# Output projection of a grouped attention as seven block products, with its weights and partial sums restaged

## The chip, the core and the metric

The kernel runs on one core of one Trainium2 chip. The metric is the device time of one execution in microseconds. A core has the engines TensorE (PE in the profile, its weight loads PEld), VectorE (DVE), ScalarE (ACT), GpSimd (POOL) and SyncE (SP, which here only issues DMAs).

## The reference

One block works on x of 1024 tokens by 512 channels, all float32: x plus attention A (32 heads of 16), plus a feed-forward with routed low-rank experts, plus attention B, plus the same feed-forward again. The change lies in attention B, which has 32 query heads and 8 key/value heads of 128 channels:

```python
q = (x @ Wq.T).reshape(b, s, H, HD).transpose(0, 2, 1, 3)
k = (x @ Wk.T).reshape(b, s, HKV, HD).transpose(0, 2, 1, 3)
v = (x @ Wv.T).reshape(b, s, HKV, HD).transpose(0, 2, 1, 3)
q = _rmsnorm(q, q_norm_w)
k = _rmsnorm(k, k_norm_w)
...
attn = jax.nn.softmax(scores + bias[None], axis=-1)
out = jnp.einsum('bkgqs,bksd->bkgqd', attn, v)
out = out.reshape(b, H, s, HD).transpose(0, 2, 1, 3).reshape(b, s, H * HD)
return out @ Wo.T
```

The mask is causal, with a slope per head. The last line, `out @ Wo.T`, is the output projection: 1024 x 4096 times 4096 x 512.

## The kernel before, in words

Attention B (`attention_b`, from L743) walks over 8 groups g, one per key/value head, with four query heads hh each. For one head, `softmax` (L1070) makes eight row tiles of 128 queries, i from 7 down to 0. A tile's scores go by PE into the two score banks (`s`, L1079, up to 1024 columns in pieces of 512), DVE adds scale and bias (L1081) and takes the maximum (L1085), ACT makes the exponentials (L1088), DVE the reciprocal of the sum (L1090), POOL the division (L1091). Two tiles later (`LAG = 2`) `columns` has DVE transpose the tile in 32x32 blocks (L1106, L1112). After a head's last tile, `product` (L1154) has PE multiply by v into the four banks `o` in strips of 32 partitions (L1140); the part of keys 512 to 1023 of all four heads is done once per group in `product_rest` (`or`), at the third tile of the next group. ACT copies the result to `oT` (L1173), 128 channels by 1024 tokens for each head, in five buffers.

All other PE work of attention B is cut into units and mixed between the tiles. The main loop (L1266 on) lets a tile's PE work be followed by as many units as `due` says, from the table `SHARE`. n counts the 32 tiles of a group. A unit is always worth one 128x512 product, which is two PE instructions in float32. In group g these run, in this order (`parts`):
- `project_kv(g + 1)`, 14 units: k and v of the next group, 128-column products (L920). With x and the weights cut into 2 x 2 blocks, `seven` (L868) makes four block products out of seven; ACT copies two of the seven out of PSUM (L880, L883), DVE adds the other five (L888), and POOL makes the sums of weight blocks that serve as weights (L862, L865, L881, L884). The next product into a bank has to wait until the previous one was read out, and the order `STEADY` leaves another product between the two.
- `project_o(g - 1)`, 32 units (L760): for each of eight token tiles four 128x512 products, summed in one bank over the four heads (L765). ACT copies each sum to one of two slots (`stage`, L772), and POOL issues a DMA that adds it to the running sum xd in HBM (L773). For the last group there is no xd; its two halves are added to x directly (L779, L781).
- `project_q(g + 1, r)`, 14 units for each pair r of heads: 512-column products (L993), `seven` as above.

The two banks `m` (`ps_m`) serve all units, the transposes of k and the sums of squares. `sum_ready` and `square` form the scale of each query head: ACT squares (L1035), PE sums (L1057), DVE transposes (L1063) and scales (L1067), POOL takes the power (L121). They run after `project_kv` and at the ends of heads.

Weights have a buffer each: `wkv` (512 KB, L797), `wq` (1 MB, L807) and `wo` (1 MB, L814), loaded on SP's queue a group ahead. SP also makes the 32 copies of v per group (L909). The units of a group end with the group (`for _ in fill` at L1326); group 0 has 42, the others 74.

Of the kernel before, what the change touches and what calls it, by code (L numbers as in the profile page):

```python
# [64 lines left out]
class Block:  # L65
# [527 lines left out]
    def load_ffn(self, pools, queue, tags, w_baseT, w_rhT, lora_B, b_base):  # L593
        w = {}
        small = pools[0].tile([P, self.FFN_SMALL], F32, tag=tags[0], name="w_small")
# [4 lines left out]
        w["base"] = pools[1].tile([P, KC, C], F32, tag=tags[1], name="w_base")  # L600
# [142 lines left out]
    def attention_b(self, ctx, wo_pool, WqT, WkT, WvT, WoT, qw, kw, xnT, xd, missing, ffn_weights):  # L743
# [12 lines left out]
        stage = beside[:, 3]  # L756
        wp = ctx.enter_context(tc.tile_pool(name="b_w", bufs=1))
        oTs = {}

        def project_o(g, wo, heads, ps_m, tag, spare=None):  # L760

            for t in range(NT):
# [7 lines left out]
                if g < HKV - 1:  # L770
                    to, rows = stage[:, t % 2], xd[t * P : (t + 1) * P, :]
                    nc.scalar.copy(to, ps)  # L772
                    nc.gpsimd.dma_start(rows, to, accum_op=ALU.add)  # L773
                    if g == HKV - 2:
                        if t == 0:
                            self.hold(self.xp, "o")
                        nc.sync.dma_start(self.x[t], rows)
                elif spare is None:
                    nc.vector.tensor_add(self.x[t], self.x[t], ps)  # L779
                else:  # L780
                    nc.scalar.copy(spare[:, t % 2], ps)  # L781
                    add = nc.gpsimd.tensor_tensor(self.x[t], self.x[t], spare[:, t % 2], ALU.add)
                    if t >= NT - 2:

                        tc.keep_in_program_order(add)
                yield

        with ExitStack() as ctx:
# [7 lines left out]
            def load_kv(g, pinned=False):  # L796
                wkv = wp.tile([P, KC, 2, DB], F32, tag="wkv", name=f"wkv{g}")  # L797
# [8 lines left out]
            def load_q(g, pinned=False):  # L806
                wq = wp.tile([P, KC, GRP * DB], F32, tag="wq", name=f"wq{g}")  # L807
                dma = nc.sync.dma_start(wq, WqT[:, g * GRP * DB : (g + 1) * GRP * DB].rearrange("(k p) n -> p k n", p=P))
# [10 lines left out]
            wkv, wq = load_kv(0, pinned=True), load_q(0, pinned=True)  # L819
# [37 lines left out]
            def weight_forms(w, name, pinned=True):  # L857
# [3 lines left out]
                s2 = work.tile([P, H, DB], F32, tag="s2", name=f"s2_{name}", bufs=3)  # L861
# [6 lines left out]
            def seven(new, multiply, left, c11, c12, c21, c22, order, done, aside=None):  # L868
# [3 lines left out]
                for m in order:  # L872
# [16 lines left out]
                    if m == 7 and aside:  # L889
                        aside()  # L890
# [20 lines left out]
            def project_kv(g, forms, aside=None):  # L911
# [21 lines left out]
                def done():  # L933
                    if not g:
                        loaded.append(load_kv(1))
# [5 lines left out]
                    for half, k_sb in enumerate(halves):  # L941
                        ssq = sm.tile([P, 4], F32, tag="ssq", name=f"ssq{g}_{half}")
                        for a in range(4):
                            sq = work.tile([P, DB], F32, tag="ksq", name=f"ksq{g}_{half}_{a}")
# [11 lines left out]
                    forms,  # L956
# [4 lines left out]
                    aside=aside,  # L961
# [15 lines left out]
            def q_forms(g, wq, r):  # L977
                return weight_forms(wq.rearrange("p k (n d) -> p k n d", d=DB)[:, :, 2 * r : 2 * r + 2], f"q{g}_{r}", g > 0)

            ahead = {}  # L980

            def project_q(g, wq, r, new=None):
# [33 lines left out]
                if g:  # L1016
                    if not r:
                        ahead[g, 1] = q_forms(g, wq, 1)
                    if later:
                        k_columns(*later.pop(0))  # L1020
# [3 lines left out]
                    ahead.pop((g, r)),  # L1024
# [19 lines left out]
            loaded = []  # L1044

            def sum_squares(g, hh, sq_T, behind):
# [15 lines left out]
                by_token = work.tile([P, NT, B], F32, tag="st", name=f"by{g}_{hh}", bufs=1)  # L1062
# [131 lines left out]

            def boundary():
# [5 lines left out]
            wo = load_o(0)  # L1201
            with tc.high_priority(offset=400):
                kv_forms = weight_forms(wkv, "kv0", False)
                for r in range(2):
                    ahead[0, r] = q_forms(0, wq, r)
            front = ps_o.tile([P, NB, QC], F32, tag="o", name="front")
            kv = project_kv(0, kv_forms)
            q0 = project_q(0, wq, 0, lambda m: ps_s.tile([P, QC], F32, tag="s", name=f"pq0_0_{m}"))
            q1 = project_q(0, wq, 1, lambda m: front[:, 2 if m == 6 else 3])
# [20 lines left out]
            forms = weight_forms(loaded[0], "kv1")  # L1230
            pending = []
            fill = iter(())
# [32 lines left out]

            for g in range(HKV):  # L1266
# [3 lines left out]
                parts = [fill] if last else []  # L1270
                if not last:
                    wq = load_q(g + 1)
                    parts.append(project_kv(g + 1, forms, lambda g=g + 1, wq=wq: ahead.update({(g, 0): q_forms(g, wq, 0)})))
                if g:
                    parts.extend((boundary(), project_o(g - 1, wo, heads, ps_m, "m")))
                    parts.extend(() if last else (project_q(g + 1, wq, r) for r in range(2)))
                else:
                    parts.extend((project_q(1, wq, 0), boundary(), project_q(1, wq, 1)))
                fill = in_turn(*parts)

                units = 42 + 32 * (g > 0)
                done = share = 0
                for hh in range(GRP):
                    if g < HKV - 2:
                        if hh == 2:
                            wkv = load_kv(g + 2)
                        elif hh == 3:
                            forms = weight_forms(wkv, f"kv{g + 2}")
# [207 lines left out]
```

## Time and profile before

| what | value |
|---|---|
| median of the runs | 1570.91 us (1570.74 to 1570.96) |
| profiled execution, own time | 1571.58 us |
| its span, first to last instruction | 1569.8 us |
| granted TensorE clock | 0.999 |
| PE, PEld busy | 98%, 59% |
| DVE, ACT, POOL busy | 67%, 42%, 29% |
| L765, output projection of attention B | 512 instructions, 237.9 us busy |

In the profile, an instruction's group shows its busy time and mean duration, then the idle time of its engine before it and what ended that. Matmuls overlap, so that the mean duration of one (593 ns for 128x512 in L765) is longer than the step from one start to the next. The timeline shows starts, and the table of windows gives busy time per engine for chosen stretches. Groups 2 to 5 repeat every 131.1 us.

### The profile page before, as it was taken

How to read it: one execution, taken by the hardware profiler on the slowest of the kernel's cores; microseconds unless marked ns; L12 is line 12 of the kernel's file. 1: busy time of each engine (PE TensorE's matmuls, PEld its weight loads, DVE VectorE, ACT ScalarE, POOL GpSimd, SP SyncE). 2: the span in 40 equal slices, each digit the busy share in tenths (PEclk: the TensorE clock that was granted, in tenths of full speed). 3: DMA queues.
4: the chain of work that ended last, by engine and by line, in shares of the span. 5: the costliest groups of instructions: out<-in, count | busy, mean ns of one | idle time of the engine just before them, and what ended most of it. 6: DMA issues, size and time to landing. Idle time of an engine off the chain costs nothing.

```text
span 1569.8 us, 32216 instructions
## 1 busy us (share of the span) xinstructions
PE 1543.4 (98%) x12894; PEld 926.1 (59%) x12894; DVE 1058.7 (67%) x2537; ACT 662.1 (42%) x1597; POOL 463.1 (29%) x571
## 2 busy tenths in 40 slices
PE   9999999999999999999999999999999999999998
PEld 5545455555555657557656755755765675556654
DVE  4557778773566886666776667766676766776753
ACT  2216666665223544443434444343343444433430
POOL 3000000002233433432443343334244333333450
PEclk9999999999999999999999999999999999999999
DMA  5000222220033102412330331241133032135001
GB/s 208 1 1 6 20 22 19 18 20 19 29 99 95 42 1 68 68 42 55 63 60 28 82 38 31 65 72 41 54 62 61 28 69 35 34 86 122 4 2 54
DMA packets 80950, 75.34 MB, mean 48 GB/s; under 512 B 14944, under 2 KB 56672, under 8 KB 80800
## 3 DMA queue, kind: packets, MB, share of 16 engines
q1 hardware_dynamic: 70272, 52.56, 14.3%
q0 software_dynamic: 8848, 17.58, 7.7%
q10 hardware_dynamic: 1680, 3.15, 0.5%
q8 instruction: 101, 1.65, 0.5%
q14 instruction: 49, 0.40, 0.1%
HBM read 33.08 MB, written 18.87 MB: 33 GB/s over the span
## 4 chain that ended last, share of the span: by engine, by line
PE 84%; DVE 7%; POOL 4%; ACT 2%; issue 2%; SPq 0%; DMA 0%; DVEq 0%; ACTq 0%; POOLq 0%
PE s L1079 13%; PE wo L765 12%; PE o L1140 11%; PE sT L407 8%; PE pq L993 8%; PE kv L920 5%; PE oT L449 5%; PE pm_f L714 3%; PE or L1140 3%; PE s L358 3%; PE pj_v L218 2%; PE pj_q L218 2%; PE pm_ao L1370 2%; PE pj_k L218 2%; DVE p L1081 2%
## 5 line engine op out<-in xcount | busy, mean ns | idle before, releaser
L1091 POOL TENSOR_SCALAR p<-p,rs 128x1024 f32<-128x1024 f32 (+7 forms) x256 | 192.8, 754 | 407.0 <-DVE rs L1090 406.3
L1079 PE MATMUL s<-kT,qT 128*128 128x512 f32 (+3 forms) x768 | 297.0, 496 | 10.9 <-DVE p L1081 10.9
L1079 PEld LDWEIGHTS s<-kT,qT 128*128 128x128 f32 x768 | 137.9, 190 | 174.7 <-issue 114.4
L765 PE MATMUL wo<-wo,oT 128*128 128x512 f32 x512 | 237.9, 593 | 1.0 <-ACT spare L781 1.0
L1106 DVE STREAM_TRANSPOSE pT<-p 128x512 f32<-128x512 f32 (+3 forms) x256 | 152.9, 602 | 109.5 <-PE o L1140 58.8
L1088 ACT ACTIVATE p<-p,nm 128x1024 f32<-128x1024 f32 (+7 forms) x256 | 198.3, 775 | 17.9 <-ACT nm L1086 0.4
L429 ACT ACTIVATE p<-sT 128x512 f32<-128x512 f32 (+1 forms) x292 | 155.2, 593 | 89.8 <-PE s L358 35.2
L1085 DVE TENSOR_REDUCE nm<-p 128x1 f32<-128x1024 f32 (+7 forms) x256 | 188.2, 735 | 2.9
L1140 PEld LDWEIGHTS o<-pT,va 32*128 32x128 f32 x4212 | 172.9, 185 | 21.7 <-issue 10.4
L1086 ACT ACTIVATE nm<-nm 128x1 f32<-128x1 f32 x256 | 51.6, 202 | 315.6 <-DVE nm L1085 314.7
L1140 PE MATMUL o<-pT,va 32*128 32x224 f32 (+5 forms) x4212 | 181.3, 324 | 0.8 <-DVE pT L1106 0.8
L358 PE MATMUL s<-kT,qT 32*128 32x512 f32 (+3 forms) x768 | 164.4, 520 | 0.0
L407 PE MATMUL sT<-qT,kT 32*128 32x128 f32 (+3 forms) x1152 | 155.3, 401 | 0.3 <-DMA qT<-negT 0.3
L765 PEld LDWEIGHTS wo<-wo,oT 128*128 128x128 f32 x512 | 94.2, 190 | 90.7 <-issue 78.8
L1081 DVE SCALAR_TENSOR_TENSOR p<-s,rq,relr 128x512 f32<-128x512 f32 x192 | 120.9, 646 | 9.9 <-PE s L1079 9.7
L993 PE MATMUL pq<-xnTb,wq 128*128 128x512 f32 x240 | 117.8, 600 | 0.4
L1081 DVE SCALAR_TENSOR_TENSOR p<-s,rq,rel 128x512 f32<-128x512 f32 (+1 forms) x192 | 102.5, 558 | 21.0 <-PE s L1079 20.9
L407 PEld LDWEIGHTS sT<-qT,kT 32*128 32x128 f32 x1152 | 80.6, 184 | 50.6 <-issue 29.4
L1112 DVE STREAM_TRANSPOSE tT<-p 128x512 f32<-128x512 f32 (+3 forms) x128 | 63.7, 498 | 57.0 <-POOL p L1091 30.6
L375 DVE TENSOR_REDUCE part<-s 128x1 f32<-128x512 f32 x128 | 81.6, 684 | 28.1 <-PE s L358 20.1
L1090 DVE RECIPROCAL rs<-ss 128x1 f32<-128x1 f32 x256 | 39.8, 155 | 85.9 <-ACT p L1088 82.1
L508 POOL TENSOR_TENSOR o<-o,over 64x512 f32<-64x512 f32 x12 | 15.3, 1272 | 270.1 <-DMA o<-oTs 224.0
(201 smaller groups left out, 2161.8 us busy)
## 6 DMA issues: line engine op xcount, KB each, us to landing
va<-v SPq DMA_DIRECT2D x256, 64.0 KB
xd<-beside POOLq DMA_DIRECT2D x56, 256.0 KB, 4.1
wq<-in_b_WqT_dram SPq DMA_DIRECT2D x8, 1024.0 KB
wo<-in_b_WoT_dram SPq DMA_DIRECT2D x8, 1024.0 KB
x_x<-in_x_dram SPq DMA_DIRECT2D x8, 256.0 KB
wkv<-in_b_WkT_dram SPq DMA_DIRECT2D x8, 256.0 KB
xd<-x_x ACTq DMA_DIRECT2D x8, 256.0 KB
wkv<-in_b_WvT_dram SPq DMA_DIRECT2D x8, 256.0 KB
```

What stands on the lines that cost most here:

```text
L358: nc.tensor.matmul(made[j][:, at:end], lhsT=qT[rows_of(j), c, i * P : (i + 1) * P], rhs=kT[rows_of(j), c, kc * QC : kc * QC + end - at], s ...
L407: nc.tensor.matmul(made[j][:, at:end], lhsT=kT[rows_of(j), c, b * P : (b + 1) * P], rhs=qT[rows_of(j), c, qc * QC + x0 : qc * QC + x1], st ...
L429: nc.scalar.activation(p[:, j, :end], made[j][:, :end], AF.Exp)
L765: nc.tensor.matmul(ps, lhsT=oTs[g, h][:, t * P : (t + 1) * P], rhs=wo[:, h, :], start=(h == heads[0]), stop=(h == heads[-1]))
L993: ins = nc.tensor.matmul(ps, lhsT=w[:, kc, :], rhs=x[:, kc, :], start=first and kc == 0, stop=kc == H - 1, skip_group_check=True,)
L1079: nc.tensor.matmul(s, lhsT=qT[:, i * P : (i + 1) * P], rhs=kT[:, lo:hi], start=True, stop=True)
L1081: nc.vector.scalar_tensor_tensor(p[:, lo:hi], s, rq[:, i : i + 1], rels[i % 2][:, at + lo : at + hi], ALU.mult, ALU.add)
L1085: nc.vector.tensor_reduce(nm, p[:, :w], AX.X, ALU.max, negate=True)
L1088: nc.scalar.activation(p[:, :w], p[:, :w], AF.Exp, bias=nm, scale=slope, accum_out=ss)
L1091: nc.gpsimd.tensor_scalar(p[:, :w], p[:, :w], rs, 1.0, ALU.mult, ALU.mult)
L1106: nc.vector.transpose(PT[:, i : i + (NT - 1) * (m - 1) + 1 : NT - 1, :], p[:, : m * P].rearrange("p (j k) -> p j k", k=P))
L1140: nc.tensor.matmul(cols(o[:, a], j, j + skip), lhsT=vs[g][j // 4][rows, j % 4 * NB + b, :], rhs=moving(j, j + skip, rows, slice(b * B, (b ...
```

## The change

`project_o` stays for the last group alone. For the others, `project_all(g, r)` makes the output projection in two halves r. Each takes two token tiles of the first 512 tokens and two of the second as the two rows of a 2 x 2 block matrix; heads 0, 1 and heads 2, 3 are its columns, and the weights are cut into 256 by 256 blocks. Seven block products of four 128x256 matmuls each take the place of eight. DVE forms the sums of blocks of `oT` in place (`combine`, `s1`), POOL forms four sums of weight blocks per group (`give_o`, into `more`). The first product is kept in SBUF (`first`), three more are copied to two slots by ACT, three are added to `first` by DVE, and six DMAs per half add the results to xd. The seven use two `m` banks, in the order 1, 5, 2, 6, 3, 7, 4, with products 1 and 2 in one tile, then 6, 7 and 4 in another, and 5 and 3 in a third.

The weights of kv and of the two pairs of q come in tiles of 512 KB that share two buffers (`wp`, tag `w`), so that the two pairs of q are loaded one by one; `give` makes the weight sums, at tiles given by number. The units form one queue that goes on from group to group: in a group come the 28 units of `project_all(g - 1)`, then kv, then the first pair of q, then the second. Group 0 runs 33 units and the others 70, so that nine units of each second pair fall into the group that uses it.

Besides, `s2` has two buffers in place of three and `ksq` one in place of two, the transposed sums of squares lie in the squares' own tile, and the feed-forward's weights share one tile, the one that `beside` had. `aside` is gone.

```diff
...
-        stage = beside[:, 3]
-        wp = ctx.enter_context(tc.tile_pool(name="b_w", bufs=1))
+        wp = ctx.enter_context(tc.tile_pool(name="b_w", bufs=2))
...
-                if g < HKV - 1:
-                    to, rows = stage[:, t % 2], xd[t * P : (t + 1) * P, :]
-                    nc.scalar.copy(to, ps)
-                    nc.gpsimd.dma_start(rows, to, accum_op=ALU.add)
...
+                wkv = wp.tile([P, KC, 2, DB], F32, tag="w", name=f"wkv{g}")
...
-            def load_q(g, pinned=False):
-                wq = wp.tile([P, KC, GRP * DB], F32, tag="wq", name=f"wq{g}")
-                dma = nc.sync.dma_start(wq, WqT[:, g * GRP * DB : (g + 1) * GRP * DB].rearrange("(k p) n -> p k n", p=P))
+            def load_q(g, r, tile=None, pinned=False):
+                wq = tile or wp.tile([P, KC, 2, DB], F32, tag="w", name=f"wq{g}_{r}")
+                n0 = (g * GRP + 2 * r) * DB
+                dma = nc.sync.dma_start(wq, WqT[:, n0 : n0 + 2 * DB].rearrange("(k p) (n d) -> p k n d", p=P, d=DB))
...
-            wkv, wq = load_kv(0, pinned=True), load_q(0, pinned=True)
+            wts = {(0, "kv"): load_kv(0, pinned=True), (0, 0): load_q(0, 0, pinned=True)}
+            wts[0, 1] = load_q(0, 1, pp.tile([P, KC, 2, DB], F32, tag="p", name="wq0_1"), pinned=True)
...
+
+            def give(g, what, pinned=True):
+                forms[g, what] = weight_forms(wts.pop((g, what)), f"{g}_{what}", pinned)
...
+            more = work.tile([P, 3, 2, C // 2], F32, tag="wo", name="wo_forms", bufs=1)
+            first = work.tile([P, 2, C // 2], F32, tag="m1", name="first", bufs=1)
+            slots = [beside[:, 3, n].rearrange("p (t n) -> p t n", t=2) for n in range(2)]
+            outer = {}
+
+            def give_o(g):
+                wo = wos[g]
+                y11, y12, y21, y22 = (wo[:, j : j + 2, k : k + C // 2] for j in (0, 2) for k in (0, C // 2))
+                t2, t3, t4 = (more[:, n] for n in range(3))
+                add = nc.gpsimd.tensor_tensor(y12, y12, y11, ALU.subtract)
+                tc.keep_in_program_order(add)
+                nc.gpsimd.tensor_tensor(t2, y22, y12, ALU.subtract)
+                nc.gpsimd.tensor_tensor(t3, t2, y11, ALU.subtract)
+                nc.gpsimd.tensor_tensor(t4, y21, t2, ALU.subtract)
+                outer[g] = {1: y11, 2: y21, 3: y22, 4: t4, 5: y12, 6: t2, 7: t3}
+
+            def project_all(g, r):
+
+                y = outer[g]
+                cols = [slice(h * QC + 2 * r * P, h * QC + 2 * (r + 1) * P) for h in range(2)]
+                x11, x12, x21, x22 = ([oTs[g, h][:, cols[n]] for h in hs] for n in range(2) for hs in ((0, 1), (2, 3)))
+                x = {1: x11, 2: x12, 3: x12, 4: x22, 5: x21, 6: x11, 7: x11}
+
+                def combine(to, a, b, op):
+                    for t, u, v in zip(to, a, b):
+                        nc.vector.tensor_tensor(t, u, v, op)
+
+                def send(i, k, of):
+                    rows = slice(i * QC + 2 * r * P, i * QC + 2 * (r + 1) * P)
+                    to = xd[rows, k * (C // 2) : (k + 1) * (C // 2)].rearrange("(t p) n -> p t n", p=P)
+                    nc.gpsimd.dma_start(to, of, accum_op=ALU.add)
+
+                if not r:
+                    for h in range(2):
+                        s1 = oTs[g, h][:, QC:]
+                        nc.vector.tensor_add(s1, s1, oTs[g, h + 2][:, QC:])
+                held[0] = True
+                for n, m in enumerate((1, 5, 2, 6, 3, 7, 4)):
+                    if m in (1, 5, 6):
+                        ps = ps_m.tile([P, 2, C // 2], F32, tag="m", name=f"wo{g}_{r}_{m}")
+                        if m == 5:
+                            other = ps
+                        else:
+                            main = ps
+                    ps = other if m in (5, 3) else main
+                    for t in range(2):
+                        for h in range(2):
+                            nc.tensor.matmul(
+                                ps[:, t, :],
+                                lhsT=x[m][h][:, t * P : (t + 1) * P],
+                                rhs=y[m][:, h, :],
+                                start=m in (1, 5, 6) and not t and not h,
+                                stop=h == 1,
+                                skip_group_check=True,
+                            )
+                        if not t:
+                            yield
+                    to = slots[n % 2]
+                    if m == 1:
+                        nc.scalar.copy(first, ps)
+                        combine(x11, x21, x11, ALU.subtract)
+                    elif m in (5, 2, 3):
+                        nc.scalar.copy(to, ps)
+                        send(*{5: (1, 1), 2: (0, 0), 3: (0, 1)}[m], to)
+                        if m == 2:
+                            combine(x12, x12, x11, ALU.subtract)
+                    elif m in (6, 7):
+                        nc.vector.tensor_add(to, first, ps)
+                        send(*{6: (0, 1), 7: (1, 1)}[m], to)
+                        if m == 6:
+                            combine(x11, x22, x11, ALU.subtract)
+                    else:
+                        nc.vector.tensor_add(first, first, ps)
+                        send(1, 0, first)
+                        held[0] = False
+                        if g == HKV - 2:
+                            if not r:
+                                self.hold(self.xp, "o")
+                            for t in (2 * r, 2 * r + 1, 2 * r + NT // 2, 2 * r + NT // 2 + 1):
+                                nc.sync.dma_start(self.x[t], xd[t * P : (t + 1) * P, :])
+                    yield
...
+            queue = []
+
+            def fill():
+                while queue:
+                    if next(queue[0], queue) is not queue:
+                        return True
+                    queue.pop(0)
...
-                parts = [fill] if last else []
-                if not last:
-                    wq = load_q(g + 1)
-                    parts.append(project_kv(g + 1, forms, lambda g=g + 1, wq=wq: ahead.update({(g, 0): q_forms(g, wq, 0)})))
                 if g:
-                    parts.extend((boundary(), project_o(g - 1, wo, heads, ps_m, "m")))
-                    parts.extend(() if last else (project_q(g + 1, wq, r) for r in range(2)))
+                    queue.append(boundary())
+                    queue.extend(project_all(g - 1, r) for r in range(2))
+                if last:
+                    queue.append(boundary())
                 else:
-                    parts.extend((project_q(1, wq, 0), boundary(), project_q(1, wq, 1)))
-                fill = in_turn(*parts)
-
-                units = 42 + 32 * (g > 0)
+                    queue.extend((project_kv(g + 1), project_q(g + 1, 0), boundary(), project_q(g + 1, 1)))
+                units = 70 if g else 33
                 done = share = 0
                 for hh in range(GRP):
-                    if g < HKV - 2:
-                        if hh == 2:
-                            wkv = load_kv(g + 2)
-                        elif hh == 3:
-                            forms = weight_forms(wkv, f"kv{g + 2}")
-                    if g and hh == 2:
+                    if not last:
+                        if g and not hh:
+                            wts[g + 1, "kv"] = load_kv(g + 1)
+                        if hh == 1:
+                            wts[g + 1, 0] = load_q(g + 1, 0)
+                            if g:
+                                give(g + 1, "kv")
+                        if hh == (3 if g else 2):
+                            wts[g + 1, 1] = load_q(g + 1, 1)
+                        if hh == 3:
+                            give_o(g)
+                    if hh == 2:
...
                         n = hh * NT + at + 1
+                        if not last and n == (2 * NT + 1 if g else NT + 4):
+                            give(g + 1, 0)
+                        if not last and n == (3 * NT + 4 if g else 2 * NT + 5):
+                            give(g + 1, 1)
                         if not last:
                             share += SHARE[i]
-                            due = min(units * share // (GRP * sum(SHARE)), units - 2 * (g == HKV - 2))
-                            if g and n <= 3 * NT + LAG:
-                                due = min(due, units - 7 * H)
-                                if n == 3 * NT + LAG:
-                                    due = units - 7 * H
+                            due = units * share // (GRP * sum(SHARE))
+                            for hh_, edge in enumerate((23, 37) if g else ()):
+                                if n == (hh_ + 1) * NT + LAG:
+                                    due = edge
                         elif hh < 2:
-                            due = 2 + max(0, (n - 2) * 32 // 14)
+                            due = 37 * n // (2 * NT)
                         else:

-                            due = 34 + max(0, 14 * (n - 19) // 13)
+                            due = 38 + max(0, 14 * (n - 19) // 13)
...
```

## The prediction

> **What bounds the kernel.** I read first the page's busy times, then windows, one per head (eight tiles) of a steady group, then the timeline of PE, and last the rows of single operations.
>
> ```profile
> PE 1543.4 (98%) x12894; PEld 926.1 (59%) x12894; DVE 1058.7 (67%) x2537; ACT 662.1 (42%) x1597; POOL 463.1 (29%) x571
> ```
>
> Busy PE is not PE at its peak, so the windows must say whether anything else limits it. Columns: stretch; length, then busy time (and instructions) of PE, PEld, DVE, ACT, POOL; clock; DMA share; GB/s. The first four are heads 1, 2, 3 of a steady group and head 0 of the next; the last two are heads of group 0.
>
> ```profile
> 889.50:919.90 30.40, 30.40 (x200) 16.91 (x199) 20.13 (x43) 15.41 (x42) 12.06 (x14) 1.00 0.46 76
> 919.90:949.90 30.00, 30.00 (x201) 16.77 (x200) 19.62 (x40) 11.55 (x29) 12.88 (x16) 1.00 0.35 69
> 949.90:982.10 32.20, 31.30 (x203) 17.26 (x202) 24.43 (x52) 13.49 (x33) 10.77 (x14) 1.00 0.00 1
> 982.10:1020.60 38.50, 38.16 (x397) 30.48 (x396) 26.65 (x60) 14.58 (x47) 12.47 (x15) 1.00 0.25 67
> ...
> 513.17:537.26 24.09, 22.47 (x188) 14.16 (x187) 20.54 (x46) 13.80 (x43) 11.89 (x16) 1.00 0.26 67
> ...
> 565.00:588.85 23.85, 23.45 (x177) 13.82 (x176) 19.75 (x41) 9.79 (x26) 8.25 (x12) 1.00 0.00 1
> ```
>
> The reader is to see that PE idles 0 us where DVE is busy 65 to 66% (heads 1 and 2, where the output projection runs with no work of DVE), 0.9 us at 76%, and 0.4 and 1.6 us at 83 and 85%. So PE bounds, and DVE is the next bound, close behind.
>
> ```profile
> 914.27 0.81 PE L1079 MATMUL s<-kT,qT 128*128 128x384 f32 x2
> 914.92 1.88 PE L765 MATMUL wo<-wo,oT 128*128 128x512 f32 x4
> 916.63 0.59 PE L1079 MATMUL s<-kT,qT 128*128 128x256 f32 x2
> 917.06 1.02 PE L765 MATMUL wo<-wo,oT 128*128 128x512 f32 x2
> 917.92 0.38 PE L1079 MATMUL s<-kT,qT 128*128 128x128 f32 x2
> 918.14 1.88 PE L765 MATMUL wo<-wo,oT 128*128 128x512 f32 x4
> ```
>
> From start to start, four 512-column instructions take 1.71 us, 0.429 each; two of 256 take 0.43, 0.215 each; two of 128 take 0.22. Price goes by columns, with fresh weights each time.
>
> **PE, the gain.** A group's projection was 8 token tiles x 4 heads x 2 instructions = 64, at 0.429 = 27.4 us. It becomes 2 halves x 7 products x 4 matmuls x 2 = 112, at 0.215 = 24.1 us: 3.3 us less. Seven groups give **23 us**. Kv and q keep their instructions; nine units move from group 0 to the last, which is no change of PE's work.
>
> **DVE, added beside PE.** Rows of the same kinds:
>
> ```profile
> L888 DVE TENSOR_TENSOR qT<-qT,pq 128x512 f32<-128x512 f32 x50 | 33.3, 667 | 0.0
> L855 DVE TENSOR_TENSOR xnTb<-xnTb x4: 392/404/946, 448.6 to 459.9; 128x256 f32<-128x256 f32 x4
> L632 POOL TENSOR_TENSOR x_x<-x_x,w_small x8: 1264/1269/1273, 379.0 to 411.4; 128x512 f32<-128x512 f32 x8
> L773 POOL DMA_DIRECT2D xd<-beside x56: 873/890/986, 630.0 to 1441.0; - x56
> DMA to landing us min/median/max: 3.8/4.1/6.3
> ```
>
> Per group: 2 `s1` at 0.67, 12 `combine` at 0.40, 6 adds from PSUM at 0.67 = 10.2 us. By heads, with the new units: head 0 loses kv's five adds (3.4) and gains four of q, `s1`, six combines and one add (7.1): 30.4 of 38 us, 80%. Head 1 gains six combines and four adds (5.1): 25.2 of 29.6, 85%. Head 2 gains kv's adds and one more (4.0): 23.6 of 29.5, 80%. Head 3 stays at 76%. Head 1 is thus where group 0's heads are, at 0.4 to 1.6 us of idle PE each, where it had none. With it the others rise a little. I take 0.6 us per group, **+4 us** over seven; the ends are 0 and two heads at 1.6, 22 us.
>
> The 392 to 946 ns of L855 are the same add alone and beside POOL's weight sums. [...] At 0.9 in place of 0.4, twelve combines would be 6 us more of DVE per group, and the sum by it would lie at the slow end of the range, near that of the slower rival below.
>
> **Banks.** Products 2 and 6, and 7 and 4, follow each other in one bank, so PE must wait between them: for ACT's copy (0.58, L772) or DVE's add (0.67), each after a tail of 0.16 (593 less 429 ns). By the new `due`, 2 and 6 meet in one tile in both halves; 7 and 4 are parted by the product of head 0 (5.5 us) in the first half and by the next tile's scores (1.7 us) in the second, so they cost nothing. Between 2 and 6 only the scores of a small tile (0.22 to 0.43 us) can stand in. That leaves about 0.4 us each: 0.8 per group, **+5.5 us**. Ends: 0, and all four bare, 2 x 0.74 + 2 x 0.83 = 3.1 per group, 22 us. Queued behind a late add on DVE are the next tile's L1081 and with them the score banks.
>
> **Group 0** loses nine units, 9 x 0.858 = 7.7 us of PE, and four adds, 2.7 us of DVE. It had 82.9 us of DVE in 100; it would have 80.2 in 92.3, 87%. PE idles 4 us there now; I take 2.5 more, **+2.5 us** (0 to 7.7).
>
> **Costed at nothing.** POOL gains four weight sums of 1.27 and four sends of 0.89 per group, 8.6 us on 48 of 131: the division is late by at most the four sums, 5.1 us, and two tiles (7 us) lie between it and `columns`. [...] Slots come round after two products, 7 us, against a copy, an issue and a landing, 5.6. `first` is taken again by the next half after head 0's product and two tiles. If a tile's time shrinks, ACT waits, and the exponentials behind it; at 1 us each this is 7 us. ACT keeps eight copies per group. The scale of the next group's head 0 is formed two tiles before its use rather than six: squares, sums, transpose and power take 1.06 + 0.64 + 0.41 + 0.13 + 1.66 = 3.9 us; five units and three small tiles, 5.6 us, cover it; if not, 1 us per group. The x tiles and the feed-forward's weights are reloaded some 60 us before use.
>
> **SP.** The 16 copies of the first half of v stand in front of the load of the second pair's weights:
>
> ```profile
> 863.50 31.18 SPq L909 DMA_DIRECT2D va<-v  x32
> 894.79 0.54 SPq L799 DMA_DIRECT2D wkv<-in_b_WkT_dram  x1
> ```
>
> 16 x 0.97 = 15.6 us, and some 5 us for 512 KB (1 MB of `wo` moved within the 10 us after 939.7): the weights lie there 20 us after kv is done, just when POOL comes to their sums (n = 28, about 20 us by units and tiles). The units need them 4 us later. I take 0; behind POOL's wait stand the divisions.
>
> **Sum.** -23 + 4 + 5.5 + 2.5 = -11 us on the profiled execution's 1571.6 gives 1560.6; the median lies 0.7 lower, so **1560 us**.
>
> **Rivals.**
> 1. All of PE's gain comes through: other ready work fills the bank waits, as in heads 1 and 2 now. 1571 - 23 = 1548, up to 1553. For it: PE idles only 1.2 of 131 us per group now. Against: DVE at 85%.
> 2. DVE becomes the bound of heads 0 and 1, and PE stands at the score banks: slower from 2.9 us of new idle time per group ((23 - 2.5) / 7). Two heads at 1.6 and three bare bank waits at 0.8 are 5.6 per group: 39 + 2.5 - 23 = +18.5, 1589; at 4.0 per group it is 1578. For it: the heads of group 0 and the range of L855.
> 3. The second pair's weights land late. Each us that POOL is held beyond the 4 us of cover costs a us in six groups; at 2 us, 12, the gain is gone: about 1571.
> 4. The products don't run at the 256-column price. The 0.215 of the scores, with its own weight load each, speaks against that; I give it nothing.
>
> **Chances.** Forecast (1554 to 1567) 0.49, full gain 0.14, no change 0.12, slower 0.25. A time within 0.2%, 3 us, can't be told from no change. So faster 0.63, same 0.12, slower 0.25. Leaving one in ten out on either side, the range is 1549 to 1586; the forecast's own is 1554 to 1567.
>
> **What would show it.** The projection's line 112 instructions per group at 0.215 from start to start; the step of a group 131.1 to about 129; DVE at 85% in head 1 and PE idle there under 1 us; PE waiting on `first` or slot copies after product 2, and not after 7; POOL waiting for a landing before product 3's send; group 0 shorter by 5 us. The prediction is wrong if PE's waits on L1081 grow past 3 us per group, or if POOL waits for `wq`.

## The result, and the profile after

The changed kernel takes 1633.92 us (median of 4 runs, 1631.58 to 1634.18); the kernel before took 1570.93 beside it. The ratio is 1.0394, with a 95% interval of 1.0376 to 1.0412: 63 us slower, where 11 us less was forecast, and far outside the range. The profiled execution took 1633.97 us, of which the span is 1632.2.

The page's row of busy times, after:

```profile
PE 1547.9 (95%) x13230; PEld 993.8 (61%) x13230; DVE 1115.7 (68%) x2677; ACT 664.7 (41%) x1597; POOL 555.2 (34%) x627
```

PE has 336 more instructions and is busy 4.5 us longer, in a span 62.4 us longer: its share fell from 98 to 95%. One steady group shows it more closely. It is taken here from the first matmul of `or` (`product_rest`) to that of the next group, in the timeline of PE. The windows, before and then after; the columns are those of the prediction's windows:

```profile
998.70:1129.80 131.10, 129.86 (x997) 81.42 (x996) 90.83 (x193) 55.04 (x149) 48.17 (x58) 1.00 0.26 53
```

```profile
1019.70:1157.30 137.60, 129.89 (x1045) 90.92 (x1044) 99.26 (x213) 55.38 (x148) 61.55 (x66) 0.99 0.31 58
```

The 48 additional matmuls are there (112 for 64). PE's idle time went from 1.2 to 7.7 us. The clock is 0.99 in place of 1.00, and PE's busy time didn't fall. By the same marks groups 1 to 5 take 137.6, 139.2, 142.3, 137.6 and 139.7 us (each 131.1 before), group 6 takes 141.4 (125.8), and the last 75.3 (62.0). By the unrounded marks these are 40.6 + 15.6 + 13.3 us more; ahead of the first mark 4.6 us are won and behind the last one 2.5. The sum is 62.4, the whole difference of the two spans.

The list of waits says what PE stood for. Columns: who waited, for what; us in all, times, longest.

```profile
PE wo L1228 <- DVE beside L1248: 39.5, 12, 7.2
DVE beside L1248 <- DMA xd<-beside: 37.9, 13, 6.9
POOL xd L1211 <- issue: 36.2, 7, 8.0
ACT beside L1243 <- DMA xd<-beside: 17.7, 7, 3.0
PE s L1065 <- DVE p L1067: 15.4, 25, 1.5
```

Read from the second line up: VectorE's add of a product into a staging slot (L1248) waits for the landing of the send that still reads this slot, and PE waits for that add. POOL's 36.2 us have no releaser in the list, but POOL's own semaphore instructions on L1211 last up to 8242 ns: POOL stands at a send. The score banks, which the prediction feared, went only from 10.9 to 15.4 us; their line before was:

```profile
PE s L1079 <- DVE p L1081: 10.9, 19, 1.6
```

The second half of a projection, in the timeline of PE:

```profile
924.69 1.89 PE L1228 MATMUL wo<-wo_forms,oT 128*128 128x256 f32 x8
926.42 1.89 PE L1228 MATMUL wo<-wo,oT 128*128 128x256 f32 x8
928.14 0.39 PE L1065 MATMUL s<-kT,qT 128*128 128x128 f32 x2
929.03 2.00 PE L1228 MATMUL wo<-wo_forms,oT 128*128 128x256 f32 x8 [0.50 <-DVE beside L1248]
930.87 1.88 PE L1065 MATMUL s<-kT,qT 128*128 128x512 f32 x4
938.59 2.08 PE L1228 MATMUL wo<-wo_forms,oT 128*128 128x256 f32 x4 [5.85 <-DVE beside L1248]
```

and of POOL, DVE and SP over the same stretch:

```profile
929.28 1.21 POOL L1211 DMA_DIRECT2D xd<-beside  x1 [1.78 <-DVE rs L1076]
930.06 1.51 POOL L1077 TENSOR_SCALAR p<-p,rs 128x384 f32<-128x384 f32 x2
938.26 2.46 POOL L1211 DMA_DIRECT2D xd<-beside  x2 [6.69 <-issue]
939.78 1.36 POOL L1077 TENSOR_SCALAR p<-p,rs 128x128 f32<-128x128 f32 x1
...
937.85 0.69 DVE L1248 TENSOR_TENSOR beside<-first,wo 128x512 f32<-128x512 f32 x1 [5.59 <-DMA xd<-beside]
...
928.34 0.37 SPq L807 DMA_DIRECT2D wo<-in_b_WoT_dram  x1
```

Products 6, 3 and 7 begin at 924.69, 926.42 and 929.03; the first two are 1.73 us apart, 0.216 per instruction. Product 3 is the last that reads the old `wo`, so at 928.34 SP starts the load of the next 1 MB. Product 6's sum is sent at 929.28 into that load and lands 8.5 us later. Until then two things stand still: VectorE before product 7's add, which takes the same slot (937.85), and POOL before product 3's send, which adds to the same bytes (938.26), with the division of the next tile (939.78) behind it. PE stands for the first of the two until 938.59, before product 4, which goes on in product 7's bank.

The sends of the changed kernel (L1211), from issue to landing:

```profile
DMA to landing us min/median/max: 4.1/4.4/9.8
```

Product 6's send of the second half takes 6.3, 7.1, 8.5, 6.9, 8.1 and 9.8 us in groups 1 to 6.

### The profile page after: what moved, and what is told of

Its sections match the earlier page's. It is cut to its first block, busy times and chain, and to the rows that moved or that the text cites. A ratio compares the mean times of both kernels' runs of the same rounds, so it can differ in the third digit from the quotient of the medians.

```text
span 1632.2 us, 33202 instructions
## 1 busy us (share of the span) xinstructions
PE 1547.9 (95%) x13230; PEld 993.8 (61%) x13230; DVE 1115.7 (68%) x2677; ACT 664.7 (41%) x1597; POOL 555.2 (34%) x627
## 4 chain that ended last, share of the span: by engine, by line
PE 65%; DVE 14%; POOL 7%; ACT 5%; DMA 5%; issue 3%; SPq 0%; DVEq 0%; ACTq 0%; POOLq 0%
PE o L1126 9%; PE s L1065 8%; PE sT L407 7%; PE pq L983 7%; DMA xd<-beside 5%; PE wo L1228 5%; PE oT L449 5%; DVE nm L1071 3%; PE or L1126 3%; POOL p L1077 3%; PE pm_f L714 3%; DVE p L1067 3%; ACT p L1074 3%; PE s L358 3%; DVE pT L1092 2%
## 5 line engine op out<-in xcount | busy, mean ns | idle before, releaser
L1077 POOL TENSOR_SCALAR p<-p,rs 128x1024 f32<-128x1024 f32 (+7 forms) x256 | 220.7, 868 | 327.6 <-DVE rs L1076 300.3
L1065 PE MATMUL s<-kT,qT 128*128 128x512 f32 (+3 forms) x768 | 304.6, 506 | 15.6 <-DVE p L1067 15.4
L1092 DVE STREAM_TRANSPOSE pT<-p 128x512 f32<-128x512 f32 (+3 forms) x256 | 152.0, 600 | 74.5 <-POOL p L1077 39.5
L1228 PE MATMUL wo<-wo_forms,oT 128*128 128x256 f32 x336 | 91.4, 415 | 39.7 <-DVE beside L1248 39.5
L1211 POOL DMA_DIRECT2D xd<-beside x70 | 89.0, 1331 | 76.5 <-issue 36.2
L1228 PE MATMUL wo<-wo,oT 128*128 128x256 f32 x448 | 105.7, 381 | 1.8 <-ACT first L1240 1.2
L1228 PEld LDWEIGHTS wo<-wo_forms,oT 128*128 128x128 f32 x336 | 66.4, 206 | 66.1 <-DVE beside L1248 46.5
```

The source lines that it names most:

```text
L1065: nc.tensor.matmul(s, lhsT=qT[:, i * P : (i + 1) * P], rhs=kT[:, lo:hi], start=True, stop=True)
L1077: nc.gpsimd.tensor_scalar(p[:, :w], p[:, :w], rs, 1.0, ALU.mult, ALU.mult)
L1092: nc.vector.transpose(PT[:, i : i + (NT - 1) * (m - 1) + 1 : NT - 1, :], p[:, : m * P].rearrange("p (j k) -> p j k", k=P))
L1228: nc.tensor.matmul(ps[:, t, :], lhsT=x[m][h][:, t * P : (t + 1) * P], rhs=y[m][:, h, :], start=m in (1, 5, 6) and not t and not h, stop=h ...
```

## The experiments

**Landing theory** (L where an expectation shortens it): product 6's send lands late because `wo`'s load runs beside it, and the landing is waited for in two places, by the slot and by the same-bytes send. **Rivals**: the density of VectorE's work; and W, the rest of the change (shared weight buffers, moved units). Ratios are to the kernel before beside each run.

### One user of the landing taken away: e1_third_slot, e2_second_sum

```diff
...
-                    to = slots[n % 2]
+                    to = slots[n % 3]
...
```

The third slot takes the room of one of v's three buffers.

> A third staging slot (v has two buffers in place of three to make room), so that product 7's add takes the slot of product 2 and not that of product 6. Theory L (the landing of product 6's send holds DVE's add of product 7, and PE behind it): PE's wait on that add falls from 39.5 us to under 8, the clock's half-speed spells in the groups go with it (16 us of loss), and the time falls from 1634 to 1570 to 1590; POOL is still held at product 3's send, which is why I don't expect less. Rival D (VectorE is too busy in heads 0 and 1): nothing changes, 1628 to 1636. Rival W (the weights in two shared buffers come late): nothing changes, 1628 to 1636.

Measured 1624.5 us (1621.3 to 1627.8), ratio 1.0341 (1.029 to 1.039): the expectation missed by 35 us. PE's wait for L1248 is gone, and another stands in its place:

```profile
POOL xd L1212 <- issue: 34.3, 7, 6.8
PE o L1126 <- DVE pT L1092: 25.0, 6, 5.3
```

POOL is held as long as before (34.3 for 36.2 us); the divisions behind its send come late, the transposes of them (L1092) too, and PE waits for these. The time fell by 9 us only. The slot is then the first of two waits for one landing; the runs with both taken away test this.

```diff
...
-                        send(*{5: (1, 1), 2: (0, 0), 3: (0, 1)}[m], to)
+                        send(*{5: (1, 1), 2: (0, 0), 3: (0, 1)}[m], to, xd if m == 2 else xe)
...
```

> Products 5 and 3 are sent to a second running sum in HBM, so that no two sends of a half add to the same bytes and POOL has no landing to wait for; slots as in the changed kernel. The second sum is left out of the output. Theory L with the slot as the place: product 7's add still waits for product 6's landing, so the time stays within 10 us of 1634, and only POOL's hold (5 to 8 us before product 3's send) goes. If POOL's hold by the same bytes is the place: PE's wait on the add goes and the time falls to 1575 to 1600. Rivals D and W: 1628 to 1636.

Measured 1639.2 us (1637.6 to 1640.9); what goes to `xe` is left out of the output. Filling `xe` ahead of group 0 delays its start by 8.6 us, so the groups are hardly different from the changed kernel's. POOL's stand without a releaser falls from 36.2 to under 1 us, and PE still waits 36.6 us for L1248, in 10 places: with the same-bytes wait gone, the slot alone holds PE.

### Both taken away: e5_third_second, e6_third_second_late

> The changed kernel with both users of the late landing taken away at once: a third staging slot, and products 5 and 3 sent to a second sum in DRAM, so that no send adds to bytes that another send of the same half has in flight (the second sum is left out of the output; it is filled once in group 0). Landing theory: the third slot alone left POOL's hold, the second sum alone left the slot; with both gone neither PE nor POOL waits for product 6's landing, the step of a group falls from 139.6 to 131 to 134 us and the time to 1575 to 1595. Rival, VectorE's density (more sums on it than it can hide): none of its work is gone, so the time stays at the better of the two single edits, 1620 to 1630.

The run has the two edits above together. Measured 1592.7 us (1592.65 to 1592.78), ratio 1.0143. In its list of waits PE no longer stands for the slot's add nor POOL for anything without a releaser, and the groups take 132.1 to 133.4 us, as expected. Group 0 starts 10 us late here (4.7 and 2.0 of it are PE's waits for `wkv` and `wq`, behind the filling of `xe`, in spite of its later place), so an estimate without that is some 1583 us. Density would have left the time at 1620 to 1630.

> As the run before, and the load of wo and its sums one head later. Landing theory: nothing waits for the landing any more, so where the load lies no longer matters for the projection: within 10 us of the run before, 1570 to 1590. If the load also slows something else (reads of the copies of v, the weights behind it), it is more than 15 us faster than that run. Density theory: 1600 to 1610, as the later load alone gave 1604.6.

Measured 1588.4 us (1587.0 to 1589.9), 4.3 less than the run before: within the 10 us that the landing theory gave.

### The load moved or taken away: e3_late_wo, e11_small_wo

```diff
...
-                        if hh == 3:
+                        if g and hh == 3:
+                            wos[g] = load_o(g)
+                        if not g and hh == 3:
                             give_o(g)
...
-                        if g:
+                        if last:
                             wos[g] = load_o(g)
...
+                        if g and not last and n == 4 * NT - 1:
+                            give_o(g)
...
```

The load is kept in program order behind the copies of v.

> The 1 MB of output weights is loaded behind the copies of v in head 3 and not as soon as its buffer is free, which is beside product 6's send of the second half; the weight sums follow at the group's last tiles. Theory L says that this load stretches the landing from 4.3 us to 6.3 to 9.8 us: the landing returns to 4.5, PE's wait on the add falls by 3 to 4 us per group, 1634 falls to 1590 to 1610. If the landing is long for another reason, it stays at 6 to 10 us and the time above 1628. Rivals D and W: 1628 to 1636.

Measured 1604.6 us (1603.9 to 1605.2), ratio 1.0214. Product 6's send now lands in 4.1 to 4.3 us in groups 1 to 6 (6.3 to 9.8 in the changed kernel). In the last group the load stays where it was, and that send still takes 7.5 us, the longest of all:

```profile
DMA to landing us min/median/max: 4.1/4.2/7.5
```

The wait for L1248 falls to less than half, not to nothing:

```profile
PE wo L1230 <- DVE beside L1250: 15.6, 10, 4.4
```

```diff
...
+                if 0 < g < HKV - 1:
+                    nc.sync.dma_start(wos[g - 1][:, :, :16], whole[:, :, :16])
+                    return wos[g - 1]
...
```

> The changed kernel with 1/32 of wo's load for groups 1 to 6, at the same place (the rest of wo is that of the group before; the sums on wo stay). Landing theory with the load as the cause: product 6's send lands in 4 to 5 us, the waits on line 1248 fall from 5 to 7 us to under 2 per group, and the time is 1585 to 1605, like that of the later load (1604.6) or better. Rival, the send is slow by itself (its issue takes 1.21 us and its pieces are 1 KB): the landing stays over 6 us and the time at 1625 or more.

Measured 1607.2 us (1606.0 to 1608.3), 2 us above the upper end. The landing is 4.1 to 4.3 us in groups 1 to 6 and PE's wait is 15.8 us, as with the later load (2.3 per group, where under 2 was expected). So it is the load, not the send by itself, that makes the landing late, and its price is 27 to 29 us; with a landing of 4.2 us two slots are still too few.

### VectorE's sums left out: e10_no_sums

```diff
...
                 def combine(to, a, b, op):
-                    for t, u, v in zip(to, a, b):
-                        nc.vector.tensor_tensor(t, u, v, op)
+                    return
...
-                if not r:
-                    for h in range(2):
-                        s1 = oTs[g, h][:, QC:]
-                        nc.vector.tensor_add(s1, s1, oTs[g, h + 2][:, QC:])
...
```

> The changed kernel without the twelve combinations per group and the two sums before them (6.1 us of VectorE per group; the block sums of the attention output are left out of the products). Landing theory: PE's wait for the score banks falls by at most the 0.5 us per group that it rose, so 1627 to 1636. Density theory: VectorE is back below its load before the change, and the time falls under 1600.

Measured 1628.9 us (1627.7 to 1630.0), 5 us less than the changed kernel. PE's wait at the score banks didn't fall (17.1 us in 25 places, against 15.4), and its wait for the slot's add stayed at 34.9. Density as the main cause falls.

### The rest of the change alone: e4_old_o

The new queue, weights and buffers with the old `project_o` (64 matmuls, eight copies and sends per group); units 74, edges 25 and 41.

> The output projection as before the change (32 units, two slots, eight sends), in the new queue of units with the two shared weight buffers (74 units, edge at 41). Theory L: the rest of the change costs little, 1568 to 1580. Rival W: 1600 or more, with POOL or PE waiting for wq or wkv. Rival D says the same as L here, since VectorE loses the ten us per group.

Measured 1589.6 us (1587.8 to 1591.4), ratio 1.0119 (1.009 to 1.0148): between the two. Without any of the seven products the rest costs 19 us, which the prediction put at 2.5. By the marks above: start -5.0, groups 1 to 5 +1.0 each, group 6 +6.3 and the last +10.6 (both do units that group 0 did before), the end +2.9. One wait of the last group is new:

```profile
PE wo L765 <- DMA wo<-in_b_WoT_dram: 3.7, 1, 3.7
```

The last `wo` arrives late there; this wait is in the list neither of the changed kernel nor of the next ones, so that the 19 us are not a part of the 63 as they stand.

### Fewer sends: e7_merged, e8_merged_late

The blocks are summed in SBUF and sent once: four sends per half in place of six (the expectation says seven), three slots, the whole output.

```diff
...
-                    elif m in (5, 2, 3):
+                    elif m == 5:
+                        nc.vector.tensor_add(other_sum, first, ps)
+                    elif m == 2:
                         nc.scalar.copy(to, ps)
...
+                        send(0, 0, to)
...
+                    elif m == 6:
+                        nc.vector.tensor_add(sum_, first, ps)
...
+                    elif m == 3:
+                        nc.vector.tensor_add(sum_, sum_, ps)
+                        send(0, 1, sum_)
+                    elif m == 7:
+                        nc.vector.tensor_add(other_sum, other_sum, ps)
+                        send(1, 1, other_sum)
...
```

> The changed kernel, whole output, with four sends per half in place of seven: a block's terms are added in SBUF and sent once, with a third staging slot; so no send adds to bytes in flight, and no slot is taken twice in a half. VectorE takes four reads of PSUM per group from ScalarE (2.7 us). Landing theory: as with both edits above, less three POOL issues per half: step 131 to 134 us, 1572 to 1595. Density theory: VectorE is 2.7 us per group busier, so 1634 or more.

Measured 1580.3 us (1579.9 to 1580.7), ratio 1.0064 (1.0047 to 1.0081): 54 us less than the changed kernel, with more work on VectorE.

> As the run before, and the load of wo and its sums one head later. Landing theory: within 10 us of the run before, 1565 to 1590. Density theory: about 1605 or more, as the later load alone gave 1604.6 with less work on VectorE.

Measured 1574.7 us (1574.4 to 1575.6), ratio 1.003 (1.0018 to 1.0042), the fastest version with products, and still 5 us slower than the kernel before. With six sends and two slots the later load was worth 29 us; with four sends it is worth 5.7: the load hurts mainly through the landings that something waits for.

A steady group of this kernel, whole and in four stretches (the latter by the same columns):

```profile
994.50:1126.00 131.50, 128.44 (x1049) 89.81 (x1048) 100.87 (x218) 53.39 (x144) 56.82 (x62) 1.00 0.26 53
...
994.50:1032.50 38.00, 36.76 (x345) 27.34 (x344) 29.62 (x68) 10.67 (x28) 15.73 (x16) 1.00 0.34 60
1032.50:1062.50 30.00, 30.00 (x254) 23.65 (x247) 25.05 (x56) 12.20 (x30) 15.55 (x16) 1.00 0.29 37
1062.50:1093.50 31.00, 30.04 (x254) 21.79 (x253) 23.00 (x48) 16.24 (x53) 9.99 (x14) 1.00 0.29 86
1093.50:1126.00 32.50, 31.63 (x207) 17.03 (x205) 23.20 (x49) 14.28 (x35) 15.54 (x18) 1.00 0.11 29
```

Compared with 131.1 before, the group still gains nothing. PE's busy time fell by 1.4 us, not by 3.3, and its idle time rose by 1.8 (1.24 to 3.06). By the marks above this kernel is 5.4 us ahead at the first mark, loses 1.8 in groups 1 to 5 together, 5.1 in group 6 and 4.2 in the last one, and wins 2.5 at the end: nearly all that it loses lies in the two groups that took over the moved units. Where VectorE is busy 83% (the second stretch) PE doesn't idle at all; its idle time lies at 71 to 78%.

### Two tries at the rest: e9_alternate, e12_late_k

```diff
...
-                for n, m in enumerate((1, 5, 2, 6, 3, 7, 4)):
+                for m in (1, 2, 6, 5, 7, 3, 4):
...
```

> The kernel with merged sends and the later wo, its products in the order 1, 2, 6, 5, 7, 3, 4, each in the other bank than the one before it, so that none follows in the bank of its forerunner; ScalarE's copies of products 2 and 5 become VectorE's adds (2.7 us per group more on VectorE than with merged sends). Bank theory (the 1.3 us of short gaps and the 0.5 us before the projection's line that are left per group are the waits between products of one bank): the step of a group goes from 131.5 to 129.5 to 130.5 us, 1562 to 1570, faster than the kernel before. Density theory: those gaps are VectorE's, and 2.7 us more of it makes them longer: 1575 to 1585.

Against the kernel with merged sends only product 2's copy became an add: two per group, 1.4 us of VectorE in a steady group, not 2.7. Measured 1578.1 us (1576.4 to 1580.0), ratio 1.0049. The waits in front of the projection's line are gone from the steady groups, yet a group takes 131.4 us for 131.5: PE now waits 0.66 us in each for `pT` and twice instead of once for `kT`. The end behind the last mark is 5.7 us longer. Neither theory is settled by it, since the order also moved work of ScalarE to VectorE.

```diff
...
-                if g and later:
+                if g and later and r:
                     k_columns(*later.pop(0))
...
+                    if g and not r and n == 2:
+                        k_columns(*later.pop(0))
...
```

> The kernel with merged sends and the later wo (1574.7), and the transposes of k's first half three units later, behind the first units of q instead of right behind kv. In a steady group of that kernel PE stands 0.56 us before those transposes and 0.40 us at the first bank of q behind kv's last sum. Bank theory: both waits go, about 0.9 us in six groups, 1567 to 1570, as fast as the kernel before or a little faster. Rival: the waits only move to the next thing that is late, as the other order of products showed, and the time stays within 1573 to 1576.

Measured 1577.4 us (1576.1 to 1578.7), ratio 1.0043. Both waits are gone, and another took up what they gave: the wait for the score banks, before and after this edit:

```profile
PE s L1067 <- DVE p L1069: 14.9, 19, 1.5
```

```profile
PE s L1071 <- DVE p L1073: 23.1, 30, 1.4
```

The rival held, 1.4 us above its range. No version beats the kernel before.

## Why the prediction was wrong, step by step

**The price of a product: right.** 112 instructions per group at 0.216 us.

**VectorE's density: right in size by luck, wrong in its reason.** Forecast +4 us; PE's wait for the score banks grew by 4.5 us (10.9 to 15.4). But the sums didn't make it grow: without them the wait is 17.1 us (e10_no_sums), and with the old projection 15.9 (e4_old_o). And e8_merged_late has no idle PE at 83%, so the busy share isn't the rule that the prediction made of it. The combinations take 415 ns at the median and 839 at most, near the row of 392 that the sum used. What the prediction read from L855, up to 946 ns beside POOL's weight sums, shows in the longest of them and not in the typical one: the 13 of 84 that take 647 to 839 ns all lie beside a division of POOL (27 others beside one take 398 to 443), and those beside nothing of POOL take 376 to 419.

**Banks: too high for product 2, wrong for product 4.** Between products 2 and 6 the wait was put at 0.8 us per group; in e8_merged_late it shows as 0.45. That 7 and 4 "cost nothing" failed for a reason that isn't the bank's: PE did stand right there, because product 7's add stood before its slot.

**Group 0: right.** Forecast -7.7 + 2.5 = -5.2 us, measured -4.6.

**The step that failed: what was costed at nothing about the sends.** "Slots come round after two products, 7 us, against a copy, an issue and a landing, 5.6." Both terms were wrong. Products 6 and 7 begin 4.3 us apart in the second half, where the tiles are small and the units dense: 7 us is what the prediction gave for two tiles on average. And the landing is 6.3 to 9.8 us in groups 1 to 6, since the very product that ends the use of `wo` lets SP's load of the next one start. The prediction took the 4.1 of the old sends. The row that it quoted had a maximum of 6.3 beside it, and the trace of before shows where such a landing lies: the last old send of that group goes out at 940.6, 0.9 us after the load of `wo`, and lands in 6.0 us:

```profile
939.67 0.37 SPq L815 DMA_DIRECT2D wo<-in_b_WoT_dram  x1
...
L773 POOL DMA_DIRECT2D xd<-beside x1: 889/889/889, 940.6 to 940.6; - x1
DMA to landing us min/median/max: 6.0/6.0/6.0
```

Nothing waited for it there, and so it was passed over. Of SP it asked only whether `wq` is in time. (It is: no wait for it in a steady group.)

**The same-bytes send.** The prediction named POOL's wait for a landing before product 3's send among the things to be seen, and its sum has no time for it. But the division behind that send on POOL stood too (the send at 938.26, the division at 939.78). e1_third_slot gives the price of that alone: 1624.5 us with the slot's wait gone, 9 us less than with both waits, against some 1583 (the estimate above) with neither. The wait shows as POOL's semaphore instruction of up to 8.24 us on L1211; with products 5 and 3 sent to other bytes, POOL's stands without a releaser come to under 1 us in all (e2_second_sum). In the stretch shown the wait ends with the landing, 8.5 us after the send of 929.28.

**POOL: mis-sized.** Forecast +8.6 us per group; 92 us more over seven groups are 13.2. All twelve sends of a group take 1.22 us at the median, where the sum had four more at 0.89. The new ones have two rows of 1 KB per partition, the old ones one of 2 KB; that this makes them longer was not tested.

**ScalarE's waits** for `first` and for the slots came (8.5 and 17.7 us); PE stood 1.2 us for the former.

**Left out: the clock.** The forecast knew no clock but the full one. After each of its seven stands of 3.7 to 7.2 us, one per group from group 1 on, PE runs at half speed for a while: the spells at 0.50 are 3.4 to 10.2 us long (below). They hold 30.6 us of PE's busy time; at half speed some 15 us of that are lost (an estimate), about a quarter of the 63.

**Left out: the moved units.** "No change of PE's work" is right, and yet e4_old_o shows the last two groups 17 us longer and only 5 us won at the start: work that moved out of a stretch with idle PE went into stretches with hardly any, and the last `wo` came late beside it.

**The rivals.** The slower case had the right sign with the wrong place (score banks) and at most 1589. Of the 63 us, 29 hang on the load's place beside the sends (e3_late_wo) and 54 on the sends and slots (e7_merged); the two overlap and don't add. Together they bring it to 1574.7 (e8_merged_late). Why the products' 3.3 us per group don't come through even there stays open in part: 1.8 us are new idle time of PE, in waits that moved when one of them was taken away; the other 1.9 lie within PE's busy time and weren't taken apart.

## What to carry to other kernels

Here a send that adds to DRAM kept its staging slot (VectorE waited 37.9 us for that) and, where another send to the same bytes was next, its engine's queue (up to 8.24 us) until it had landed, 4.1 to 9.8 us after its issue; cost it by the closest interval between reuse and by what else is on the DMA engines at that moment, not by the median landing and a mean tile. If two users wait for one late landing, taking one of them away shows little (9 us of 63 here): take both, or the lateness. Sum in SBUF and send once before counting on more sends.

## What the runs showed of the hardware

**The clock halved at each of the seven long stands of the changed kernel.** In one of them PE stood for 7.17 us, up to 1357.94. Windows of 3.4 us over it, the length of the shortest spells at 0.50 (657.6 to 661.0 is one); the granted clock is the column ahead of the DMA share:

```profile
1350.50:1353.90 3.40, 0.27 (x1) 0.00 (x0) 0.00 (x0) 0.25 (x2) 0.00 (x0) 1.00 0.88 195
1353.90:1357.30 3.40, 0.00 (x0) 0.00 (x0) 0.10 (x1) 0.00 (x0) 0.00 (x0) 0.50 0.16 26
1357.30:1360.70 3.40, 2.76 (x6) 1.89 (x7) 2.15 (x5) 0.00 (x0) 2.88 (x3) 0.50 0.43 46
1360.70:1364.10 3.40, 3.40 (x8) 1.99 (x6) 2.51 (x4) 1.44 (x3) 0.00 (x0) 0.50 0.86 108
1364.10:1367.50 3.40, 3.40 (x66) 3.04 (x68) 1.75 (x3) 1.09 (x2) 1.97 (x3) 0.99 0.10 5
```

The clock fell to 0.50 while PE stood and stayed there until 1364.1, for 6.2 us of PE's work; at half speed that is about 3 us lost on top of the 7.2. The stand of 5.85 us shown above (up to 938.59) was followed by 0.50 until 944.3; with the other five, of 3.72 to 5.50 us, the spell at 0.50 is 3.4 to 6.8 us long. After the window from 1357.3, with 2.76 of 3.4 us busy, the clock was still 0.50; after the next, fully busy one it was 0.99. A stand as long as these didn't always come first: in group 0 of the kernel before, a stretch of 3.41 us in which PE was busy for 1.65, with no stand longer than 1.6 us, was followed by one at half speed.

```profile
556.93:560.34 3.41, 1.65 (x14) 0.65 (x12) 3.21 (x9) 1.96 (x4) 1.49 (x2) 1.00 0.00 0
560.34:563.75 3.41, 3.41 (x11) 1.86 (x8) 2.61 (x9) 2.41 (x6) 1.65 (x1) 0.50 0.00 0
```

**A 256 KB accumulating send** (product 6's, second half) lands in 4.1 to 4.3 us without the load of `wo` beside it (e3_late_wo, groups 1 to 6) and in 6.3 to 9.8 beside this 1 MB load (the changed kernel). In the first of the five windows 195 GB/s are moved; from 1345 to 1357 the timelines of SP and POOL show no other issue than the load's (1346.47) and the send's (1347.30).
